# Rotating accumulator outputs, and sums and reciprocals planned apart, in a two-layer attention kernel

## The chip, the cores and the metric

The kernel runs on one core of one Trainium2 chip. The metric is the device time in microseconds of one launch. The core has five engines that run at the same time, each with its own queue of instructions in a fixed order: TensorE (PE) multiplies matrices, VectorE (DVE) and ScalarE (ACT) work on elements, GpSimd (POOL) too, and SyncE (SP) starts transfers. Semaphores tell one engine that another has finished, and an engine can also wait on its own.

## The reference

The input x has 8 batches of 1024 tokens (64 by 16) with 128 channels. Two layers follow each other.

```python
# layer 0: 8 heads; the softmax over m, then another one over g, of the same scores
scores = einsum('bhlfc,bhmgc->bhlfmg', q, k) / sqrt(c)
a = softmax(scores, axis=4)
a = softmax(a, axis=5)
z = einsum('bhlfmg,bhmgc->bhlfc', a, v)
z1 = layer_norm(z @ wo.T + bo + x)
x = layer_norm(relu(z1 @ w1.T + b1) @ w2.T + b2 + z1)
# layer 1, attention: additive scores, a tanh of every pair of tokens
Wi = B @ W.T                      # B: the normalised tokens
scores = einsum('d,bijd->bij', v, tanh(Wi[:, None] + Wi[:, :, None]))
t = t + softmax(scores, axis=-1) @ B
# layer 1, recurrence over the tokens
y_t = sigmoid(wx_t + y_{t-1} @ V)
```

The tanh of all pairs (1024 x 1024 x 128 for each of 8 batches, of which the symmetry lets the kernel compute about half) is the largest piece of work for ScalarE.

## The kernel before

Everything up to the recurrence is a list of operations, given to a small scheduler, the class `Plan`, which is part of the kernel's Python program. An operation has one or several engines that can do it, each with a price in microseconds written by hand (`add(("DVE", 1.49), first_sums, ...)`), the keys that it reads and writes, and a priority that acts as a due time in units of batches. `emit` runs through a simulated time and fixes, before anything runs on the chip, the order of each engine's instructions and, where there is a choice, the engine. At each step it takes the engine that can start first, at the time `first`, and then the operation of lowest priority value among those which can start on it by `first + slack`, with `slack=0.15`. An operation can start when its engine is free and all that it depends on is done, plus a delay: the table `LATENCY` if the other operation ran on another engine, the table `AGAIN` (line 500) if it ran on the same one.

Layer 0 works on tiles of 128 queries by 1024 keys, 64 tiles for each batch (8 heads by 8 tiles). The steps of a tile are: the scores on PE (L939) into one of two score buffers `sc`; the exponential on ACT (L942); on VectorE `first_sums`, one Python function with a `tensor_reduce` over m (L946) and a `reciprocal` of the 16 sums (L947); then `divide` (L950), which writes into a buffer `e` and sets the score buffer free. After each second tile there follow, for both together, the second exponential on ACT (L960), and on VectorE `second_sums`, with the reduction over g (L963) and a `reciprocal` of 128 sums (L964). GpSimd divides by them (L974), PE transposes (L853), VectorE copies the transposes out of PSUM (L865), and PE multiplies with the values (L988). There are two buffers `e` for pairs of tiles. `stat_e` holds the sums.

Layer 1's additive scores are computed in groups of rows (function `group`). A row is one token i against the tokens j: the matrix `wiT` plus one of its columns, then tanh, then a product with v on PE (L1175). ACT can do sum and tanh in one instruction for each row (L1097). Or GpSimd (L1107) or VectorE makes the sums, and ACT takes the tanh of many rows in one wide instruction (L1155). On VectorE a group of fewer than 4 rows is made row by row by `add_row` (L1101), a `tensor_scalar` with two additions and an accumulator output. That output is not used; it goes to `unused`, one column of the small tile `stats[5]`, the same for all rows. The scheduler chooses for each group which engine fills it; these rows are the work with which it fills ACT, VectorE and GpSimd. The sums lie in a ring in the tile `th`, whose room comes free when PE has used it.

Layer 0 of batch b+1 runs beside layer 1 of batch b, so that the first batch's layer 0 stands alone at first, and the last batch's layer 1 is alone at the end. After all batches the recurrence runs in chunks.

Of the kernel before, what the change touches and what calls it, by code (L numbers as in the profile page):

```python
# [11 lines left out]
ALU = mybir.AluOpType  # L12
# [3 lines left out]
P = 128  # L16
# [466 lines left out]
class Plan:  # L483
# [13 lines left out]


    LATENCY = {"PE": 0.6, "ACT": 0.5, "DVE": 0.4, "POOL": 0.6, "SP": 8.0}
    AGAIN = {"PE": 0.0, "ACT": 0.0, "DVE": 0.08, "POOL": 0.15, "SP": 8.0}  # L500

    def __init__(self):
        self.ops = []
# [130 lines left out]
def fast_path(ctx: ExitStack, tc: tile.TileContext, a: dict, fits):  # L634
# [22 lines left out]
    work = main.enter_context(tc.tile_pool(name="work", bufs=1))  # L657
    psum = main.enter_context(tc.tile_pool(name="psum", bufs=1, space=PSUM))

    def tile_of(pool, name, shape):  # L660
        return pool.tile(shape, F32, tag=name, name=name)
# [132 lines left out]
    add = plan.add  # L794
# [5 lines left out]
    stats = ring("stat", 7, [P, 4, 9])  # L800
# [36 lines left out]
    count = {"aT": 0}  # L837
# [34 lines left out]
    def layer0(b):  # L872
# [16 lines left out]
        for n_part, part in enumerate(parts):  # L889
# [3 lines left out]
            for h in range(H):  # L893
                L0 = pace(n_part, h)

                u, vp, kvp = us[h % 2], vps[h % 2], ("vp", h % 2)
                if alone:
                    vp, kvp = th[:, (12 + h) * N : (13 + h) * N].rearrange("p (t c) -> p t c", c=C), ("vp0", h)
                for s in range(2) if part is None else (part,):
                    cols = slice(s * 512, (s + 1) * 512)  # L900

                    def project(bank, h=h, cols=cols):
                        nc.tensor.matmul(bank, A[:, h, :], xT[:, cols], start=True, stop=True)  # L903

                    def biased(e, bank, h=h, u=u, cols=cols):
                        if e == "ACT":
                            nc.scalar.activation(u[:, cols], bank, AF.Identity, bias=ub[:, h : h + 1])
                        else:
                            nc.vector.tensor_scalar(u[:, cols], bank, ub[:, h : h + 1], None, ALU.add)

                    through_bank(project, 0.9, [kx], biased, evict(0.75), [], [("u", h % 2, s)], L0, banks)
                for s in () if alone and n_part else range(2):

                    def values(bank, h=h, s=s):
                        for i in range(4):
                            t = 4 * s + i
                            nc.tensor.matmul(  # L917
                                bank[:, i * P : (i + 1) * P], xT[:, t * P : (t + 1) * P], Wvo[:, h, :], start=True, stop=True
                            )

                    through_bank(
                        values, 0.95, [kx], copy(vp[:, 4 * s : 4 * s + 4, :]), evict(0.68), [], [kvp + (s,)], L0, banks
                    )
                for qt in qts:
                    L0 = pace(n_part, h + (qt - qts[0]) / len(qts))
                    i = (n_part * H + h) * len(qts) + qt - qts[0]
                    sc, kc = scs[i % 2], ("sc", i % 2)
                    pair, q = (b * H * NT + i) // 2 % NE, qt % 2
                    e2, st = es[pair], stat_e[pair]
                    e, ke = e2[:, q, :], ("e", pair, q)  # L930
                    k1, k2 = ke + (1,), ("e", pair, 2)
                    r1, r2 = st[:, q, 0:G], st[:, :, G : G + M]
                    sc3 = sc.rearrange("p (m g) -> p m g", g=G)
                    e3 = e.rearrange("p (m g) -> p m g", g=G)

                    def scores(_, sc=sc, u=u, qt=qt):
                        for s in range(2):
                            cols = slice(s * 512, (s + 1) * 512)
                            nc.tensor.matmul(sc[:, cols], u[:, qt * P : (qt + 1) * P], xT[:, cols], start=True, stop=True)  # L939

                    add(("PE", 1.74), scores, r=[kx, ("u", h % 2, qt // 4)], w=[kc], pri=L0)
                    add(("ACT", 0.98), lambda _, sc=sc: nc.scalar.activation(sc, sc, AF.Exp, scale=SCALE),  # L942
                        r=[kc], w=[kc], pri=L0)

                    def first_sums(_, sc=sc, r1=r1):
                        nc.vector.tensor_reduce(r1, sc.rearrange("p (m g) -> p g m", g=G), AX.X, ALU.add)  # L946
                        nc.vector.reciprocal(r1, r1)  # L947

                    def divide(_, e3=e3, sc3=sc3, r1=r1):
                        nc.vector.tensor_tensor(e3, sc3, r1.unsqueeze(1).to_broadcast([P, M, G]), ALU.mult)  # L950

                    add(("DVE", 1.49), first_sums, r=[kc], w=[k1], pri=L0)
                    add(("DVE", 1.22), divide, r=[kc, k1], w=[ke], pri=L0)
                    if q == 0:
                        continue


                    ks = [("e", pair, q) for q in range(2)]
                    L0 -= DOWN
                    add(("ACT", 1.9), lambda _, e2=e2: nc.scalar.activation(e2, e2, AF.Exp), r=ks, w=ks, pri=L0)  # L960

                    def second_sums(_, e2=e2, r2=r2):
                        nc.vector.tensor_reduce(r2, e2.rearrange("p q (m g) -> p q m g", g=G), AX.X, ALU.add)  # L963
                        nc.vector.reciprocal(r2, r2)  # L964

                    add(("DVE", 3.25), second_sums, r=ks, w=[k2], pri=L0)
                    na = next_aT()
                    aT = aTs[na]
                    for q in range(2):
                        e, ke = e2[:, q, :], ("e", pair, q)  # L970

                        def divide_again(_, e=e, r2=r2, q=q):
                            e3 = e.rearrange("p (m g) -> p m g", g=G)
                            nc.gpsimd.tensor_tensor(e3, e3, r2[:, q, :].unsqueeze(2).to_broadcast([P, M, G]), ALU.mult)  # L974

                        add(("POOL", 1.97), divide_again, r=[ke, k2], w=[ke], pri=L0)
                        for s in range(2):
                            through_bank(
                                transposes([e[:, t * P : (t + 1) * P] for t in range(4 * s, 4 * s + 4)]), 0.52, [ke],
                                copy(aT[:, 4 * s : 4 * s + 4, q * P : (q + 1) * P]), evict(0.68), [],  # L980
                                [("aT", na, q, s)], L0, banks,
                            )
                    q0 = (qt - 1) * P
                    bank = Bank(*banks)

                    def attend(part, vp=vp, aT=aT, bank=bank):
                        for t in range(4 * part, 4 * part + 4):
                            nc.tensor.matmul(bank()[:, :256], vp[:, t, :], aT[:, t, :], start=t == 0, stop=t == NT - 1)  # L988

                    def gather(_, h=h, q0=q0, bank=bank):  # L990
                        zq = zs[:, q0 : q0 + 2 * P]
                        if h == 0:
                            nc.vector.scalar_tensor_tensor(zq, bank()[:, :256], zb, xT[:, q0 : q0 + 2 * P], ALU.add, ALU.add)
                        else:
                            nc.vector.tensor_tensor(zq, bank()[:, :256], zq, ALU.add)

                    for s in range(2):
                        add(
                            ("PE", 1.74), lambda _, attend=attend, s=s: attend(s),
                            r=[kvp + (p,) for p in range(2)] + [("aT", na, q, p) for q in range(2) for p in range(2)],  # L1000
                            w=[("bank", bank)], pri=L0, take=None if s else bank, wait=[kz + (qt // 4,)],
                        )
                    add(("DVE", 0.42), gather, r=[("bank", bank), kx], w=[kz + (qt // 4,)], pri=L0, give=bank)

            L0 = b - 1 - SOON
            for qh in range(2) if part is None else (part,):
# [11 lines left out]
                z1T, k1 = zs[:, 512 * qh : 512 * qh + 512], kz + (qh,)  # L1018
# [51 lines left out]

                add(("POOL", 2.2), affine2, r=[kg], w=[kg], pri=L0)

    unused = stats[5][:, 3, 8:9]

    def group(it, at0, r0, k, wiT, all_wi, L1, ROWS, fillers, chain, left, both, first_half):

# [4 lines left out]
        i0 = it * P  # L1081
# [7 lines left out]
        def rows(c):  # L1089
            return slot()[:, at[c] : at[c + 1]].rearrange("p (r n) -> p r n", r=k)  # L1090

        def w_i(c, r=None):
            j = i0 + 4 * r0 + c
            return wiT[:, j : j + 4 * k - 3 : 4] if r is None else wiT[:, j + 4 * r : j + 4 * r + 1]
# [4 lines left out]
        def add_row(c, r):  # L1099

            nc.vector.tensor_scalar(  # L1101
                rows(c)[:, r, :], wiT[:, i0 + begin[c] :], w_i(c, r), 0.0, ALU.add, ALU.add, accum_out=unused
            )

        def add_rows(eng, c):
# [472 lines left out]
```

## Time and profile before

| | |
|---|---|
| median of 3 runs | 5390.36 us (5388.69 to 5394.67) |
| the profiled execution | 5390.73 us, its span 5388.9 us |
| reductions L946 / L963 | 512 x 1.212 us / 256 x 2.278 us |
| reciprocals L947 / L964 | 512 x 0.253 us / 256 x 0.953 us |
| divide L950 | 512 x 1.219 us |
| rows on VectorE, L1101 | 1822, mean 0.871 us, and an accumulator read of 0.083 us each |
| rows on ACT, L1097 | 2056, mean 0.782 us |
| wide tanh on ACT, L1155 | 971, mean 2.771 us |
| rows on GpSimd, L1107 | 2304 instructions, mean 1.486 us (VectorE has 80 of this line besides) |

A time in the profile is the time at which an engine worked on an instruction. The records of two instructions of one engine can overlap a little. "Idle before" is what lay free on the engine before an instruction starts, with the engine (and its line) whose signal ended the wait. A fixed order means that an engine whose next instruction waits does nothing else in the meantime.

### The profile page before, as it was taken

What the parts mean: (1) busy time and instruction counts of PE and PEld (TensorE: products, weight loads), DVE (VectorE), ACT (ScalarE), POOL (GpSimd) and SP (SyncE); (2) the same over time, 40 slices, a digit from 0 to 9 for tenths busy, and PEclk for the clock granted to TensorE, in tenths of its full rate; (3) what the DMA queues carried; (4) which work ended last, traced back from release to release, by engine and by line L of the source; (5) the groups of instructions that cost most, each with busy time, mean ns of one, the idle gap of its engine ahead of it and who ended that gap; (6) DMA issues with size and microseconds to landing.
All of it is one profiled execution on the core that took longest, in us unless ns stands there. A gap on an engine that the chain in (4) does not pass through costs nothing.

```text
span 5388.9 us, 99191 instructions
## 1 busy us (share of the span) xinstructions
PE 5048.0 (94%) x39173; PEld 2782.9 (52%) x39173; DVE 4961.5 (92%) x8448; ACT 5093.6 (95%) x4180; POOL 4536.0 (84%) x3114
## 2 busy tenths in 40 slices
PE   9999999999999999999999999999999999986567
PEld 6655555555555555555555555555555455542125
DVE  7998999999999999999999999999999999988886
ACT  5489999999999999999999999999999999999994
POOL 2364889988998899989999999989999998986992
PEclk9999999999999999999999999999999999998998
DMA  2000000000000000000000000000000000000001
GB/s 62 1 5 1 1 1 5 1 9 1 1 5 5 5 1 1 5 9 1 1 5 5 5 1 1 5 5 5 1 1 5 5 1 1 5 26 7 1 1 68
DMA packets 27339, 37.71 MB, mean 7 GB/s; under 512 B 2512, under 2 KB 19280, under 8 KB 26864
## 3 DMA queue, kind: packets, MB, share of 16 engines
q1 hardware_dynamic: 24832, 27.99, 1.6%
q8 instruction: 310, 5.08, 0.4%
q10 hardware_dynamic: 1872, 3.16, 0.2%
q14 instruction: 165, 1.35, 0.1%
q0 software_dynamic: 160, 0.13, 0.0%
HBM read 19.22 MB, written 12.06 MB: 6 GB/s over the span
## 4 chain that ended last, share of the span: by engine, by line
PE 67%; DVE 15%; ACT 12%; issue 4%; POOL 1%; DMA 0%; DVEq 0%; SPq 0%; ACTq 0%; POOLq 0%
PE sa L1175 24%; PE m L988 13%; PE sc L939 13%; PE m L853 8%; ACT th L1155 6%; DVE th L1101 6%; ACT th L1097 3%; DVE stat_e L963 2%; PE m L917 2%; PE m L1304 2%; DVE stat_e L946 2%; DVE wx L950 1%; PE m L903 1%; DVE aT L865 1%; PE m L1035 1%
## 5 line engine op out<-in xcount | busy, mean ns | idle before, releaser
L1107 POOL TENSOR_TENSOR th<-wiT 128x536 f32<-128x536 f32 (+58 forms) x2304 | 3342.3, 1486 | 244.6 <-PE sa L1175 222.8
L1155 ACT ACTIVATE th<-th 128x2740 f32<-128x2740 f32 (+54 forms) x971 | 2661.2, 2771 | 23.2 <-DVE th L1107 12.3
L1175 PE MATMUL sa<-th,vpat 128*32 128x512 f32 (+32 forms) x24576 | 2030.6, 462 | 212.5 <-ACT th L1155 187.2
L1101 DVE TENSOR_SCALAR_CACHE_REDUCE th<-wiT 128x512 f32<-128x512 f32 (+60 forms) x1822 | 1587.4, 871 | 140.1 <-PE sa L1175 21.9
L1097 ACT ACTIVATE th<-wiT 128x440 f32<-128x440 f32 (+58 forms) x2056 | 1462.7, 782 | 15.1 <-PE sa L1175 14.9
L1175 PEld LDWEIGHTS sa<-th,vpat 128*32 128x32 f32 x24576 | 662.1, 110 | 1341.8 <-issue 850.5
L974 POOL TENSOR_TENSOR wx<-wx,stat_e 128x1024 f32<-128x1024 f32 x512 | 983.2, 1942 | 403.5 <-DVE stat_e L964 360.4
L939 PE MATMUL sc<-xT,wx 128*128 128x512 f32 x2048 | 982.9, 605 | 15.7 <-DVE wx L950 15.3
L988 PE MATMUL m<-aT,wx 128*128 128x256 f32 x3584 | 829.4, 384 | 11.9 <-DVE aT L865 11.9
L988 PEld LDWEIGHTS m<-aT,wx 128*128 128x128 f32 x3584 | 671.1, 191 | 191.9 <-issue 40.7
L946 DVE TENSOR_REDUCE stat_e<-sc 128x16 f32<-128x1024 f32 x512 | 620.4, 1212 | 28.7 <-ACT sc L942 27.8
L950 DVE TENSOR_TENSOR wx<-sc,stat_e 128x1024 f32<-128x1024 f32 x512 | 623.9, 1219 | 23.3
L865 DVE COPY aT<-m 128x512 f32<-128x512 f32 x927 | 600.4, 674 | 34.5 <-PE m L853 32.1
L853 PEld LDWEIGHTS m<-ident,wx 128*128 128x128 f32 x3940 | 445.8, 141 | 326.0 <-issue 162.8
L963 DVE TENSOR_REDUCE stat_e<-wx 128x128 f32<-128x2048 f32 x256 | 583.3, 2278 | 19.0 <-ACT wx L960 18.1
L853 PE MATMUL m<-ident,wx 128*128 128x128 f32 x3940 | 564.4, 278 | 22.5 <-DVE aT L865 12.9
L942 ACT ACTIVATE sc<-sc 128x1024 f32<-128x1024 f32 x512 | 513.7, 1008 | 75.9 <-PE sc L939 71.0
L939 PEld LDWEIGHTS sc<-xT,wx 128*128 128x128 f32 x2048 | 354.9, 190 | 384.3 <-issue 331.4
L960 ACT ACTIVATE wx<-wx 128x2048 f32<-128x2048 f32 x256 | 487.2, 1903 | 21.6 <-DVE wx L950 21.3
L964 DVE RECIPROCAL stat_e<-stat_e 128x128 f32<-128x128 f32 x256 | 244.0, 953 | 8.8
L917 PEld LDWEIGHTS m<-Wvo,xT 128*128 128x128 f32 x1080 | 135.5, 193 | 47.5 <-issue 20.1
L917 PE MATMUL m<-Wvo,xT 128*128 128x128 f32 x1080 | 147.3, 282 | 6.4 <-DVE aT L865 3.0
(183 smaller groups left out, 2899.0 us busy)
## 6 DMA issues: line engine op xcount, KB each, us to landing
xT<-in_xt_dram SPq DMA_DIRECT2D x8, 512.0 KB, 3.5
th<-in_x_dram SPq DMA_DIRECT2D x8, 512.0 KB, 6.9
parked<-X SPq DMA_DIRECT2D x16, 256.0 KB, 2.3
xr<-parked SPq DMA_DIRECT2D x8, 512.0 KB, 7.7
parked_wx<-bT SPq DMA_DIRECT2D x14, 256.0 KB, 2.0
wx<-parked_wx SPq DMA_DIRECT2D x7, 512.0 KB, 3.2
out_dram<-ot ACTq DMA_DIRECT2D x8, 256.0 KB, 2.2
out_dram<-ot SPq DMA_DIRECT2D x8, 256.0 KB, 2.7
```

The source lines that it names most:

```text
L853: nc.tensor.transpose(bank[:, i * P : (i + 1) * P], s, ident)
L939: nc.tensor.matmul(sc[:, cols], u[:, qt * P : (qt + 1) * P], xT[:, cols], start=True, stop=True)
L946: nc.vector.tensor_reduce(r1, sc.rearrange("p (m g) -> p g m", g=G), AX.X, ALU.add)
L950: nc.vector.tensor_tensor(e3, sc3, r1.unsqueeze(1).to_broadcast([P, M, G]), ALU.mult)
L963: nc.vector.tensor_reduce(r2, e2.rearrange("p q (m g) -> p q m g", g=G), AX.X, ALU.add)
L974: nc.gpsimd.tensor_tensor(e3, e3, r2[:, q, :].unsqueeze(2).to_broadcast([P, M, G]), ALU.mult)
L988: nc.tensor.matmul(bank()[:, :256], vp[:, t, :], aT[:, t, :], start=t == 0, stop=t == NT - 1)
L1097: nc.scalar.activation(rows(c)[:, r, :], wiT[:, i0 + begin[c] :], AF.Tanh, bias=w_i(c, r))
L1101: nc.vector.tensor_scalar(rows(c)[:, r, :], wiT[:, i0 + begin[c] :], w_i(c, r), 0.0, ALU.add, ALU.add, accum_out=unused)
L1107: eng.tensor_tensor(rows(c), wiT[:, i0 + begin[c] :].unsqueeze(1).to_broadcast(shape), w_i(c).unsqueeze(2).to_broadcast(shape), ALU.add,)
L1155: nc.scalar.activation(slot()[:, a:z], slot()[:, a:z], AF.Tanh)
L1175: nc.tensor.matmul(sa[32 * c : 32 * c + 32, s:s1], vpat[:, 31 - r0 - r : 63 - r0 - r], rows(c)[:, r, s - at0 - begin[c] : s1 - at0 - begin ...
```

## The change

There are three edits. The accumulator outputs of `add_row` go to 16 columns of a new tile in turn. `first_sums` and `second_sums` each become two operations of the scheduler: the reduction, and the reciprocal that reads and overwrites its result; the prices become 1.15 + 0.2 for 1.49, and 2.2 + 0.9 for 3.25. The delay that the scheduler takes for an operation on VectorE which depends on another one on VectorE goes from 0.08 to 0.2.

```diff
-    AGAIN = {"PE": 0.0, "ACT": 0.0, "DVE": 0.08, "POOL": 0.15, "SP": 8.0}
+    AGAIN = {"PE": 0.0, "ACT": 0.0, "DVE": 0.2, "POOL": 0.15, "SP": 8.0}
...
                     def first_sums(_, sc=sc, r1=r1):
                         nc.vector.tensor_reduce(r1, sc.rearrange("p (m g) -> p g m", g=G), AX.X, ALU.add)
+
+                    def first_inverse(_, r1=r1):
                         nc.vector.reciprocal(r1, r1)
...
-                    add(("DVE", 1.49), first_sums, r=[kc], w=[k1], pri=L0)
+                    add(("DVE", 1.15), first_sums, r=[kc], w=[k1], pri=L0)
+                    add(("DVE", 0.2), first_inverse, r=[k1], w=[k1], pri=L0)
                     add(("DVE", 1.22), divide, r=[kc, k1], w=[ke], pri=L0)
...
                     def second_sums(_, e2=e2, r2=r2):
                         nc.vector.tensor_reduce(r2, e2.rearrange("p q (m g) -> p q m g", g=G), AX.X, ALU.add)
+
+                    def second_inverse(_, r2=r2):
                         nc.vector.reciprocal(r2, r2)
 
-                    add(("DVE", 3.25), second_sums, r=ks, w=[k2], pri=L0)
+                    add(("DVE", 2.2), second_sums, r=ks, w=[k2], pri=L0)
+                    add(("DVE", 0.9), second_inverse, r=[k2], w=[k2], pri=L0)
...
-    unused = stats[5][:, 3, 8:9]
+    unused = tile_of(work, "unused", [P, 16])
+
+    def next_unused():
+        count["unused"] = (count.get("unused", -1) + 1) % 16
+        return unused[:, count["unused"] : count["unused"] + 1]
...
             nc.vector.tensor_scalar(
-                rows(c)[:, r, :], wiT[:, i0 + begin[c] :], w_i(c, r), 0.0, ALU.add, ALU.add, accum_out=unused
+                rows(c)[:, r, :], wiT[:, i0 + begin[c] :], w_i(c, r), 0.0, ALU.add, ALU.add, accum_out=next_unused()
             )
```

## The prediction

> **What bounds the kernel now.** I read the page's busy shares first, then busy time by stage, then what ScalarE waits for in the longest stage, and last VectorE's instructions one by one. The first line of the page:
>
> ```profile
> PE 5048.0 (94%) x39173; PEld 2782.9 (52%) x39173; DVE 4961.5 (92%) x8448; ACT 5093.6 (95%) x4180; POOL 4536.0 (84%) x3114
> ```
>
> Three engines lie within three points of each other, so a mean over the span doesn't say which of them sets the end. The busy time by stage (stretch, its length, then busy us and instructions of PE, weight loads, DVE, ACT, POOL, clock, DMA) does:
>
> ```profile
> 100.00:400.00 300.00, 281.53 (x1330) 179.21 (x1329) 272.16 (x361) 189.05 (x211) 142.73 (x84) 0.99 0.01 3
> 400.00:700.00 300.00, 287.56 (x2094) 172.83 (x2093) 277.86 (x408) 291.73 (x420) 209.65 (x131) 0.99 0.00 1
> 700.00:1900.00 1200.00, 1160.74 (x8856) 635.12 (x8854) 1124.18 (x1824) 1159.99 (x846) 1066.00 (x731) 0.99 0.01 4
> 1900.00:4700.00 2800.00, 2745.94 (x21885) 1501.40 (x21882) 2644.51 (x4475) 2782.38 (x2073) 2592.13 (x1795) 1.00 0.01 3
> 4700.00:5200.00 500.00, 348.06 (x3309) 136.17 (x3311) 441.62 (x950) 489.86 (x314) 422.33 (x282) 0.93 0.03 11
> ```
>
> From 1900 to 4700 us ACT is busy 2782 of 2800 us (99.4%) and VectorE 94%; from 4700 to 5200 ACT 98%. ACT is the pacer there. Only before 400 us is ACT loose (63%), with PE at 94% and VectorE at 91%: there layer 0 of the first batch runs alone, and its chain of single steps counts. What ACT waited for in the long stage (line, releaser, total us, times, longest) leaves little to be won from VectorE directly:
>
> ```profile
> ACT sc L942 <- PE sc L939: 10.5, 13, 1.8
> ACT E L1271 <- PE sa L1175: 2.8, 3, 1.8
> ACT th L1097 <- PE sa L1175: 1.3, 2, 1.1
> ACT wx L960 <- DVE wx L950: 1.2, 2, 1.0
> ```
>
> VectorE's own time line (start, length, instruction, idle before) shows what the change aims at:
>
> ```profile
> 2516.51 0.08 DVE L1101 DVE_READ_ACCUMULATOR th<-wiT 128x1 f32 x1
> 2516.72 1.10 DVE L1101 TENSOR_SCALAR_CACHE_REDUCE th<-wiT 128x855 f32<-128x855 f32 x1
> 2517.75 0.08 DVE L1101 DVE_READ_ACCUMULATOR th<-wiT 128x1 f32 x1
> 2517.95 1.10 DVE L1101 TENSOR_SCALAR_CACHE_REDUCE th<-wiT 128x854 f32<-128x854 f32 x1
> 2518.98 0.08 DVE L1101 DVE_READ_ACCUMULATOR th<-wiT 128x1 f32 x1
> 2518.98 1.28 DVE L865 COPY wx<-m 128x512 f32<-128x512 f32 x2
> 2520.18 1.09 DVE L1101 TENSOR_SCALAR_CACHE_REDUCE th<-wiT 128x853 f32<-128x853 f32 x1
> 2521.20 0.08 DVE L1101 DVE_READ_ACCUMULATOR th<-wiT 128x1 f32 x1
> 2521.20 1.22 DVE L946 TENSOR_REDUCE stat_e<-sc 128x16 f32<-128x1024 f32 x1
> 2522.45 0.25 DVE L947 RECIPROCAL stat_e<-stat_e 128x16 f32<-128x16 f32 x1
> 2522.74 1.23 DVE L950 TENSOR_TENSOR wx<-sc,stat_e 128x1024 f32<-128x1024 f32 x1
> ```
>
> After an accumulator read a COPY or a reduction starts at the read's own start; the next row starts 0.20 to 0.21 us later. All rows write their accumulator to the one column `unused`, so each waits for the one before. The reduction, the reciprocal and the divide depend on each other too, and each starts about 0.035 us after its predecessor's end, where an independent instruction starts about 0.08 us before it (2520.18 against 2518.98 + 1.28).
>
> **What the Trainium skill says.** "VectorE: DVE Perf Modes", section "Two Vector instructions with no wait between them", counts an operation with accumulator output as two instructions; the trace agrees (1822 of each at L1101). The same page, section "The DRAIN you can't avoid", asks for a semaphore or an intervening operation where VectorE reads what it has just written, and says that the semaphore costs nothing extra. The first half fits the waits seen here. The second doesn't: 0.035 us after the end against 0.083 us before it is 0.118 us for each dependent pair, and the measurement decides. "Perfetto Trace Analysis", section "Tensor Engine Instruction (MATMUL, LD_WEIGHTS)", says that a matmul's end is estimated; so I don't take PE's 98% in the long stage as proof that PE is full.
>
> **Part 1, rotating outputs.** 1180 of the 1822 rows follow another row directly and wait on VectorE's own semaphore (counted over VectorE's records in order). Their starts lie after the accumulator read's end by 0.035 us (438 of them, that one wait), 0.12 (397, two waits) or 0.15 (344, three); without it I expect -0.083, as for the other instructions. Savings: 438 x 0.118 = 52, 397 x 0.216 (mean gap with the few true waits) = 86, 344 x 0.252 = 87: 224 us of VectorE time. A column comes round again after 16 rows, some 15 us later, so its wait costs nothing. Cover: all this is idle time of VectorE, which isn't the pacer after 400 us. The planner's row price (0.21 + 1.05e-3 w) isn't edited, so this part alone moves no row to another engine. Direct worth: nothing to ACT's load; ACT's waits on VectorE in 700 to 1900 us come to some 15 us (L1155 on L1107 9.8, on L1101 1.4, L960 on L950 3.8). I take -6, between 0 and -15.
>
> **Part 2, sums and reciprocals apart, dearer dependence.** The same instructions; L946 takes 1.212 us x512, L947 0.253 x512, L963 2.278 x256, L964 0.953 x256. With the planned delay of 0.2 us against a choice window of 0.15, the reciprocal can't be picked directly after its sums while another VectorE operation is ready. Every pair that is parted saves 0.118: 512 = 60 us; reciprocal to divide, 295 direct pairs now with 0.03 to 0.13 us gaps, 48 us; second sums, 256 = 30 us. At most 138 us of VectorE time, none where nothing else is ready.
>
> What reaches the end is the planner's new balance. It books 1.35 instead of 1.49 (512 x 0.14 = 72) and 3.10 instead of 3.25 (256 x 0.15 = 38): 110 us less on VectorE. It fills that with rows. A row taken from ACT saves ACT its fixed part only, since the tanh stays: seven rows of 610 took 4.93 us, 0.70 each; at 0.874 ns an element (L960 2048 in 1.903, L942 1024 in 1.008) 0.53 of that is the tanh, 0.17 the fixed part. For all engines to end dT earlier: rows off ACT dT/0.17 = 5.9 dT, rows off POOL dT/1.49 (L1107's mean) = 0.67 dT, each 0.95 us on VectorE (0.871 + 0.083), and VectorE itself dT shorter: 110 = dT(1 + 0.95 x 6.57) = 7.2 dT, dT = 15. The 0.08 us that the planner left idle after sums before is now filled: up to 41 us more, worth up to 6; I take 3. Sum -18; bounds 0 (all rows come off POOL) and -21.
>
> **The lone stage.** Up to 700 us there are 105 tiles. Two score buffers turn round there: a tile holds its buffer for 9.4 us (median, first score matmul to end of divide) of a cycle of 10.4 before 300 us, and 11.3 of 13.5 from 300 to 700; in the long stage only 9.1 of 17. Parting gives VectorE 0.36 us a tile (0.118, then 0.187 for the commonest gap of 0.104 before a divide plus 0.083, and half of 0.118), at best 49 x 0.36 = -18 in the part that VectorE helps to bound. But what is put between, mostly a COPY of 0.67 (0.60 with the overlap), lengthens the hold: twice 0.60 less 0.24 saved is +0.96, +0.48 a tile through two buffers, at worst 105 x 0.48 = +50. No row of before shows which wins; I take -2. Queued behind a delayed reciprocal is everything on VectorE; ACT's second exponential, PE's next scores and POOL's L974 (360 us of waits on L964 now, covered by POOL's slack) wait for it. No DMA, matmul or activation is added.
>
> Sum: -6 - 18 - 2 = -26 against the profiled 5390.7 (span 5388.9 and 1.8 around it) gives 5364.7; the median shown is 0.4 lower: 5364.
>
> **Rivals.** *VectorE's saving passes through.* The chain of waits gives VectorE 15% of the span, 808 us; shortened by 362 of 4961 (7.3%) that is -59: 5331. For it: PE waits on VectorE's copies in many small pieces. Against it: ACT's 99.4%. *Nothing arrives.* Rows come off POOL and the order reshuffles: 5390. For it: POOL has rows enough. *Slower: the score-buffer ring.* Place: layer 0 before 700 us, where hold almost equals cycle. Price: +0.48 us a tile, +50, less the 24 won later: 5416. It decides once the hold there rises by over 0.5 us (105 x 0.25 = 26, the whole gain). For it: the planner now prefers to put something between even if the tile is late. Against it: less queueing on a shorter VectorE. That the change misses its aim (waits stay since the tile and not the column is tracked) is unlikely: the reciprocal at L1308 writes the same tile as `unused` and starts directly after an accumulator read without that wait; it falls under "nothing arrives".
>
> **How the numbers follow.** Forecast 0.45 (own range 5345 to 5379), passes through 0.13, nothing 0.17, ring 0.25. Faster by over 0.2% (11 us, about what can be told from no change) 0.58, same 0.17, slower 0.25. The range takes the first rival's centre and reaches just past the ring's: 5325 to 5420.
>
> **What would show it.** Rows in sequence starting 0.08 us before the accumulator read's end; L947 seldom directly after L946; VectorE's busy share or its idle changed by 250 to 360 us in all; ACT still above 98% from 1900 us; fewer rows at L1097 than 2056 by about 90 (15/0.17). Wrong if ACT's rows don't fall, or if the hold of a score buffer before 700 us grows and ACT's full stretch begins later.

## The result and the profile after

The changed kernel takes 5317.8 us (median of 4, 5316.9 to 5319.5), 0.9869 of the kernel before (5389.5 with a fourth run; 95% interval 0.9857 to 0.9881): 72 us or 1.3% faster. The forecast was 5364, with a range from 5325. The direction was right; the gain was nearly three times the size, and the time lies 7 us below the range.

The busy line of the page after:

```profile
PE 5007.1 (94%) x39173; PEld 2763.8 (52%) x39173; DVE 4884.6 (92%) x8676; ACT 5057.1 (95%) x4042; POOL 4522.8 (85%) x3113
```

The span fell from 5388.9 to 5315.0, by 73.9 us. ACT's busy time fell by 36.5 (from 5093.6), and what is left of the span, ACT's idle time, by 37.4 (295.3 to 257.9). So, counted on ACT, half of the gain is less work and half is less waiting. VectorE's busy time fell by 77 us although it makes more rows; its share of the span is still 92%.

By stage (columns as before: stretch, length, busy us of PE, weight loads, DVE, ACT, POOL):

```profile
100.00:400.00 300.00, 276.71 (x1344) 177.77 (x1343) 276.16 (x395) 189.40 (x213) 148.73 (x87) 0.99 0.01 3
700.00:1900.00 1200.00, 1188.69 (x9224) 651.03 (x9216) 1129.55 (x1919) 1192.01 (x851) 1109.07 (x758) 1.00 0.01 4
1900.00:4700.00 2800.00, 2746.61 (x21924) 1501.89 (x21917) 2640.55 (x4659) 2779.45 (x2024) 2611.45 (x1812) 1.00 0.01 4
4700.00:5200.00 500.00, 329.15 (x3416) 119.35 (x3417) 430.57 (x1027) 499.55 (x267) 427.23 (x304) 0.97 0.02 7
```

ACT is full in more of the span: 1192 of 1200 us from 700 to 1900 (1160 before), and 499.6 of 500 after 4700 (489.9 before). The lone stage up to 400 us is as it was. The groups of rows moved like this (busy us, mean ns, then the idle time before them and what ended most of it); first VectorE's rows before, then the kernel after:

```profile
L1101 DVE TENSOR_SCALAR_CACHE_REDUCE th<-wiT 128x512 f32<-128x512 f32 (+60 forms) x1822 | 1587.4, 871 | 140.1 <-PE sa L1175 21.9
```

```profile
L1165 ACT ACTIVATE th<-th 128x2634 f32<-128x2634 f32 (+53 forms) x997 | 2734.8, 2774 | 9.3 <-DVE th L1117 6.0
...
L1111 DVE TENSOR_SCALAR_CACHE_REDUCE th<-wiT 128x344 f32<-128x344 f32 (+59 forms) x1930 | 1602.9, 867 | 68.6 <-PE sa L1185 65.8
L1107 ACT ACTIVATE th<-wiT 128x512 f32<-128x512 f32 (+62 forms) x1904 | 1369.8, 793 | 11.8 <-PE sa L1185 11.8
```

ACT does 1904 rows instead of 2056, VectorE 1930 instead of 1822. The idle time before VectorE's rows fell from 140.1 to 68.6 us, and what is left is nearly all a true wait on PE, which sets room in the ring free. VectorE's time line shows both aims of the change reached:

```profile
2503.99 1.23 DVE L946 TENSOR_REDUCE stat_e<-sc 128x16 f32<-128x1024 f32 x1
2505.13 0.94 DVE L969 RECIPROCAL stat_e<-stat_e 128x128 f32<-128x128 f32 x1
2505.99 0.20 DVE L949 RECIPROCAL stat_e<-stat_e 128x16 f32<-128x16 f32 x1
2506.11 0.98 DVE L1111 TENSOR_SCALAR_CACHE_REDUCE th<-wiT 128x829 f32<-128x829 f32 x1
2507.01 0.09 DVE L1111 DVE_READ_ACCUMULATOR th<-wiT 128x1 f32 x1
2507.10 0.42 DVE L1001 TENSOR_TENSOR zs<-m,zs 128x256 f32<-128x256 f32 x1
2507.44 1.22 DVE L952 TENSOR_TENSOR wx<-sc,stat_e 128x1024 f32<-128x1024 f32 x1
...
2521.92 1.05 DVE L1111 TENSOR_SCALAR_CACHE_REDUCE th<-wiT 128x818 f32<-128x818 f32 x1
2522.90 0.08 DVE L1111 DVE_READ_ACCUMULATOR th<-wiT 128x1 f32 x1
2522.90 1.06 DVE L1111 TENSOR_SCALAR_CACHE_REDUCE th<-wiT 128x817 f32<-128x817 f32 x1
```

Another reciprocal stands between the reduction at 2503.99 and its own at 2505.99, two other operations before its divide, and every instruction starts at or before its predecessor's end. The row at 2522.90 starts with the accumulator read of the row before it. The reduction L946 is followed directly by its reciprocal 48 times of 512, and L966 3 times of 256.

### The profile page after: what moved, and what is told of

It reads as the page before. It is cut to its first block, busy times and chain, and to the rows that moved or that the text cites. A ratio compares the mean times of both kernels' runs of the same rounds, so it can differ in the third digit from the quotient of the medians.

```text
span 5315.0 us, 98773 instructions
## 1 busy us (share of the span) xinstructions
PE 5007.1 (94%) x39173; PEld 2763.8 (52%) x39173; DVE 4884.6 (92%) x8676; ACT 5057.1 (95%) x4042; POOL 4522.8 (85%) x3113
## 4 chain that ended last, share of the span: by engine, by line
PE 67%; ACT 16%; DVE 10%; issue 6%; POOL 1%; DMA 0%; ACTq 0%; DVEq 0%; SPq 0%; POOLq 0%
PE sa L1185 25%; PE m L994 13%; PE sc L939 13%; ACT th L1165 9%; PE m L853 8%; ACT th L1107 4%; DVE th L1111 2%; PE m L1314 2%; PE m L917 2%; DVE stat_e L966 2%; PE m L903 1%; DVE stat_e L946 1%; ACT wx L963 1%; ACT sc L942 1%; DVE aT L865 1%
## 5 line engine op out<-in xcount | busy, mean ns | idle before, releaser
L1117 POOL TENSOR_TENSOR th<-wiT 128x1024 f32<-128x1024 f32 (+59 forms) x2303 | 3345.5, 1487 | 215.2 <-PE sa L1185 196.0
L1165 ACT ACTIVATE th<-th 128x2634 f32<-128x2634 f32 (+53 forms) x997 | 2734.8, 2774 | 9.3 <-DVE th L1117 6.0
L1185 PE MATMUL sa<-th,vpat 128*32 128x512 f32 (+36 forms) x24576 | 2009.0, 459 | 202.2 <-ACT th L1165 186.9
L1111 DVE TENSOR_SCALAR_CACHE_REDUCE th<-wiT 128x344 f32<-128x344 f32 (+59 forms) x1930 | 1602.9, 867 | 68.6 <-PE sa L1185 65.8
L1107 ACT ACTIVATE th<-wiT 128x512 f32<-128x512 f32 (+62 forms) x1904 | 1369.8, 793 | 11.8 <-PE sa L1185 11.8
L865 DVE COPY aT<-m 128x512 f32<-128x512 f32 x940 | 616.6, 684 | 67.6 <-PE m L853 64.3
L946 DVE TENSOR_REDUCE stat_e<-sc 128x16 f32<-128x1024 f32 x512 | 613.5, 1204 | 38.9 <-ACT sc L942 37.7
L966 DVE TENSOR_REDUCE stat_e<-wx 128x128 f32<-128x2048 f32 x256 | 583.6, 2280 | 52.5 <-ACT wx L963 51.9
L1111 DVE DVE_READ_ACCUMULATOR th<-wiT 128x1 f32 x1930 | 160.8, 83 | 0.0
```

Source lines behind the costliest of these rows:

```text
L865: nc.vector.tensor_copy(dst, src)
L1107: nc.scalar.activation(rows(c)[:, r, :], wiT[:, i0 + begin[c] :], AF.Tanh, bias=w_i(c, r))
L1111: nc.vector.tensor_scalar(rows(c)[:, r, :], wiT[:, i0 + begin[c] :], w_i(c, r), 0.0, ALU.add, ALU.add, accum_out=next_unused())
L1117: eng.tensor_tensor(rows(c), wiT[:, i0 + begin[c] :].unsqueeze(1).to_broadcast(shape), w_i(c).unsqueeze(2).to_broadcast(shape), ALU.add,)
L1165: nc.scalar.activation(slot()[:, a:z], slot()[:, a:z], AF.Tanh)
L1185: nc.tensor.matmul(sa[32 * c : 32 * c + 32, s:s1], vpat[:, 31 - r0 - r : 63 - r0 - r], rows(c)[:, r, s - at0 - begin[c] : s1 - at0 - begin ...
```

## The experiments

The theories: W, the waits of the rows are the gain; P, the scheduler's new order is, by its lower prices or by the parting; D, the longer delay alone is; and, after the first set of runs, L, much of it is the luck of one order among many. A number in the name of a "delay" or "reroll" kernel is the same-engine delay for VectorE. The kernel before was run again beside each set, with medians from 5384.4 to 5389.5 us; each ratio is to the median of its own set.

**Each part alone.** `rotate_only` is the kernel before with the rotating outputs alone, so its order is that of before. `plan_only` is the changed kernel with a single column again.

```diff
# rotate_only, against before
-    unused = stats[5][:, 3, 8:9]
+    unused = tile_of(work, "unused", [P, 16])
-  accum_out=unused
+  accum_out=next_unused()
# plan_only, against the changed kernel: the same lines the other way round
```

> Only the accumulator outputs rotate; the order of every engine stays that of the kernel before. Theory P (the gain is the scheduler's new order): VectorE isn't the pacer, so this is worth little, 5380 to 5390. Theory W (the gain is the waits of the rows that go away): most of the 72 us come here, 5325 to 5345, and ACT's idle in 700 to 1900 us falls from 40 to about 10 us. My prediction's term for it was -6, so 5384.

> The order of the changed kernel, with all rows writing one accumulator column as before. Theory P: 5318 to 5335. Theory W: the waits come back and with them most of the time, 5365 to 5385. If the two parts simply add, the gain here and that of rotate_only sum to 72 us; if the order needs the shorter rows to be kept, they sum to clearly less.

Measured: `rotate_only` 5371.8 us, ratio 0.9968 (0.9955 to 0.998), 16 us off; `plan_only` 5333.4, 0.99 (0.9883 to 0.9916), 55 off. The two add up to the 72, and the rotation is worth the same 16 us in both orders (5333.4 to 5317.8). `plan_only` lies within P's 5318 to 5335. For the rotation neither number was met: W's is too large, P's near zero too small. VectorE's rows in `rotate_only`:

```profile
2500.01 0.08 DVE L1105 DVE_READ_ACCUMULATOR th<-wiT 128x1 f32 x1
2500.01 1.10 DVE L1105 TENSOR_SCALAR_CACHE_REDUCE th<-wiT 128x861 f32<-128x861 f32 x1
2501.04 0.08 DVE L1105 DVE_READ_ACCUMULATOR th<-wiT 128x1 f32 x1
2501.15 1.11 DVE L1105 TENSOR_SCALAR_CACHE_REDUCE th<-wiT 128x856 f32<-128x856 f32 x1
```

The first row starts with the accumulator read before it; the second starts a tenth of a microsecond after its read's start, since a wait on PE is still there. Over the 1180 pairs the sum of the gaps goes from +127 to -32 us: 158 us of VectorE time, not the 224 that I had reckoned. Most of what VectorE won became waiting for others. Its rows and its copies out of PSUM, in `rotate_only` (before, 21.9 us of the idle time before the rows was ended by PE, as shown above) and then the copies before:

```profile
L1105 DVE TENSOR_SCALAR_CACHE_REDUCE th<-wiT 128x512 f32<-128x512 f32 (+60 forms) x1822 | 1500.9, 869 | 78.4 <-PE sa L1179 75.7
L865 DVE COPY aT<-m 128x512 f32<-128x512 f32 x927 | 601.4, 675 | 66.4 <-PE m L853 63.3
```

```profile
L865 DVE COPY aT<-m 128x512 f32<-128x512 f32 x927 | 600.4, 674 | 34.5 <-PE m L853 32.1
```

ACT's idle time fell by 7 us from 700 to 1900 us (40 to 33) and by 8 after 4700 (10 to 2). The second is seen in what ACT waited for from 4600 to 5300 us, before and then in `rotate_only`:

```profile
ACT th L1155 <- DVE th L1101: 5.7, 11, 1.4
ACT E L1271 <- PE sa L1175: 3.8, 3, 2.1
ACT th L1155 <- DVE th L1107: 2.5, 2, 1.5
```

```profile
ACT E L1275 <- PE sa L1179: 3.0, 3, 1.3
ACT th L1159 <- POOL th L1111: 0.4, 1, 0.4
ACT th L1159 <- DVE th L1105: 0.2, 1, 0.2
```

With layer 0 gone, the rows of the last batch follow each other on VectorE, and ACT waited 8.2 us on them (the first and the third line); it hardly does any more. ACT's busy time is nearly the same (5090.2): no row changed engine.

**Price, parting and delay.** All three have rotating outputs.

```diff
# prices_only, against rotate_only
-  add(("DVE", 1.49), first_sums, ...)
+  add(("DVE", 1.35), first_sums, ...)
-  add(("DVE", 3.25), second_sums, ...)
+  add(("DVE", 3.1), second_sums, ...)
# delay_only, against rotate_only
-  "DVE": 0.08
+  "DVE": 0.2
# split_no_delay, against the changed kernel
-  "DVE": 0.2
+  "DVE": 0.08
```

> The kernel before with rotating outputs and only the two prices lowered (1.49 to 1.35, 3.25 to 3.10), sums and reciprocals still one operation each. By my sum the lower booking alone moves rows from ACT to VectorE worth 15 us against rotate_only, with about 90 rows fewer on ACT. If rows don't move, it equals rotate_only; if the parting is what counts, also.

> Rotating outputs and the same-engine delay of 0.2; sums and reciprocals one operation each, old prices. It compares with rotate_only (5372). Theory D (the delay alone, which keeps the divide from following its sums at once, gives the time): 5335 to 5350. Theory P (parting sums and reciprocal with lower prices is needed): 5365 to 5375. It could also lose, since the planner then leaves VectorE idle for 0.2 instead of 0.08 where nothing else is ready.

> The change, but with the same-engine delay left at 0.08, which lies inside the choice window of 0.15, so that sums and reciprocal may again follow each other. Theory P in the form that parting them matters: 5335 to 5360, since up to 138 us of VectorE's waits come back. If the new prices (110 us less booked on VectorE) do it: 5315 to 5325. Theory W: 5315 to 5325 as well, since the rows rotate.

Measured: `prices_only` 5354.9 (0.9937, 0.992 to 0.9953), `delay_only` 5339.6 (0.9917, 0.99 to 0.9933), `split_no_delay` 5368.3 (0.9963, 0.9949 to 0.9977). The prices alone give 17 us against `rotate_only` where my sum had put 15, but with 180 rows fewer on ACT, not 90. The delay alone, which cuts the divides directly behind their reciprocals from 295 to 64, gives 32: theory D's 5335 to 5350. `split_no_delay`, with the same lower prices and some pairs parted (386 of 512 first pairs and 119 of 256 second ones still direct), gains almost nothing and misses all three of its expectations. Theory D fits these last two; with `prices_only` beside them no sum of mechanisms fits all three, which raised the question of chance.

**Re-rolls.** The list scheduler answers a small change of one of its numbers with another order of some 99,000 instructions. The four `reroll` kernels are `rotate_only` with other delays inside the choice window of 0.15; the five `delay` kernels with a number are the changed kernel with other delays above it. (Theory P is met by `delay_018`, `delay_022` and `delay_025`, and missed by `delay_016`, `delay_030`, `reroll_006` and `reroll_010`. `reroll_012` lies inside the range for the mechanism, `reroll_004` 3 us above it.)

```diff
# reroll_004, _006, _010, _012, against rotate_only
-  "DVE": 0.08
+  "DVE": 0.04   # or 0.06, 0.1, 0.12
# delay_016, _018, _022, _025, _030, against the changed kernel
-  "DVE": 0.2
+  "DVE": 0.16   # or 0.18, 0.22, 0.25, 0.3
```

> The changed kernel with the delay at 0.16 instead of 0.2, still just over the choice window of 0.15. Theory P (being over the window is what counts): within 10 us of the changed kernel's 5318, and sums directly before reciprocals about as seldom (48 of 512). If the 54 us between rotate_only and the changed kernel were mostly a lucky order, this one should fall anywhere between 5320 and 5370.

> rotate_only with the delay at 0.06 instead of 0.08, both inside the window: no mechanism of any theory, only another order of the same operations. The spread against rotate_only (5372) is what a new order alone can do. Theory P: within 10 us of 5372. Theory L (luck of the order): off by 20 or more.

> As reroll_006 with the delay at 0.10. Theory P: within 10 us of 5372. Theory L: off by 20 or more in either direction.

> The changed kernel with the delay at 0.18. Delays of 0.16 (5355) and 0.2 (5318) part the sums from their reciprocals alike, yet lie 37 us apart, so a sample of such orders is needed. Theory P: parted orders lie below the unparted ones (5372, 5357, 5351), so under 5345 in most. Theory L: anywhere between 5318 and 5372.

> As delay_018 with 0.25. Theory P: under 5345. Theory L: anywhere between 5318 and 5372.

> As delay_018 with 0.3. Theory P: under 5345, perhaps a little later than 0.2, since the planner books more idle time. Theory L: anywhere between 5318 and 5372.

> rotate_only with the delay at 0.04. If parted orders are better by mechanism: near the mean of the unparted ones (5372, 5357, 5351), so 5350 to 5372. If all is chance: as likely under 5340 as above.

> rotate_only with the delay at 0.12, still inside the window. As reroll_004: 5350 to 5372 by mechanism, as likely under 5340 by chance alone.

> The changed kernel with the delay at 0.22. Parted orders so far: 5355, 5343, 5318, 5321, 5352. Mechanism: 5318 to 5355, with ACT's busy time between 5043 and 5064 as in the others, against 5084 to 5090 in unparted orders with the old prices. Chance alone: up to 5372.

Measured (median us; ACT busy, and span less ACT busy, of the profiled execution, which in `reroll_004` was 10 us faster and in `delay_025` 10 us slower than the median):

| delay | unparted, old prices | ACT busy / idle | delay | parted, new prices | ACT busy / idle |
|---|---|---|---|---|---|
| 0.04 | 5375.1 | 5085.3 / 277.7 | 0.16 | 5355.3 | 5064.4 / 291.1 |
| 0.06 | 5357.4 | 5083.8 / 274.2 | 0.18 | 5343.4 | 5053.9 / 287.7 |
| 0.08 | 5371.8 | 5090.2 / 279.7 | 0.2 | 5317.8 | 5057.1 / 257.9 |
| 0.10 | 5350.8 | 5089.3 / 259.4 | 0.22 | 5321.8 | 5050.7 / 272.7 |
| 0.12 | 5363.9 | 5090.7 / 270.3 | 0.25 | 5320.7 | 5043.1 / 285.9 |
| | | | 0.30 | 5351.7 | 5052.8 / 297.1 |
| mean | 5363.8 | 5087.9 / 272.3 | mean | 5335.1 | 5053.7 / 282.1 |

What the other two edits, lower prices with the parting and the longer delay, do together is in the means: 29 us. The scatter (standard deviations 10 and 17 over 5 and 6 orders) leaves this difference uncertain by about 8 (its standard error). ACT has 34 us less to do on average, without overlap between the two columns, and idles somewhat more. The changed kernel is the best of its six, 17 below their mean, by ACT's idle time; the order of before is the second worst of its five, 8 above theirs. So theory P holds for the sign and about half of the 54 us between `rotate_only` and the changed kernel. The other half is which order came out. That it is luck, theory L, is not shown for all of it: in the right half of the table the three delays from 0.2 to 0.25 lie within 4 us of each other and the others 22 us or more above, as they would if such a delay were the best one. One order at each delay can't tell this from chance. In the left half neighbours lie 13 to 21 us apart, up and down, and there chance is the plainer reading.

**Price against parting, a second order.** `prices_010` is `reroll_010` with the prices of `prices_only`.

> reroll_010 (5351) with the two prices lowered, unparted. If the lower booking is what moves rows off ACT: ACT busy near 5063 as in prices_only, and a time some 15 us under reroll_010, 5336, give or take the scatter. If it is the parting: ACT busy near 5085 and no gain.

Measured: 5343.4 (0.9915, 0.9895 to 0.9934), 7 us under `reroll_010` (13 by the two ratios); ACT busy 5074.9, halfway between the two expectations. The two orders with new prices and no parting average 5349.2, 15 under the old prices. But `split_no_delay` has the new prices and a short delay too; with it the average is 5355.5, only 8 under, and `delay_only`, with old prices, lies 24 under. So how the 29 us divide between prices, parting and delay stays open. ACT's busy time scatters less: 5087.9 on average with old prices and a short delay, 5070.0 in the three orders with new prices and a short delay, 5075.4 in `delay_only`, 5053.7 with all. So both the prices and the delay take work off ACT.

**The row's own price.** The planner books a row on VectorE at 0.21 + 1.05e-3 w, which is now above what it takes.

```diff
# row_price, against the changed kernel
-  "DVE": lambda c: (k * (0.21 + 1.05e-3 * (w - begin[c])), ...
+  "DVE": lambda c: (k * (0.13 + 1.05e-3 * (w - begin[c])), ...
```

> The changed kernel with the planner's price of a row on VectorE lowered by 0.08 (0.21 to 0.13 + 1.05e-3 w), which is nearer to what the chip takes now that the rows follow each other without a wait. If the planner's balance sets the end, VectorE takes more rows, ACT some 100 fewer, and by the sum of the prediction (1930 x 0.08 = 154 us booked less, over 7.2) about 20 us come off: 5297. If VectorE's slack on the chip is needed to keep ACT fed, no gain or a loss: 5318 to 5340.

Measured: 5315.0 (0.9864, 0.9848 to 0.9881), the same as the changed kernel. Its busy line:

```profile
PE 5012.0 (94%) x39173; PEld 2768.7 (52%) x39173; DVE 4983.3 (94%) x9016; ACT 5033.2 (95%) x3917; POOL 4482.2 (84%) x3085
```

ACT lost 24 us of work, about as reckoned (148 rows less), and got 23 us of idle time in its place. Of this 16 us are waits of its second exponential on VectorE's divide, in the changed kernel and then here:

```profile
ACT wx L963 <- DVE wx L952: 15.6, 12, 3.4
```

```profile
ACT wx L963 <- DVE wx L952: 31.5, 15, 6.0
```

That the busier VectorE costs what the lighter ACT gains would fit this. But the idle time of ACT is 280.6 us here, as in the average parted order (282.1); it was the changed kernel that had little. Against the mean of its kind, 5335.1, `row_price` is 20 us faster, just what was reckoned. One order doesn't decide between the two readings.

**A cause of the scatter.** In `delay_016` ACT's wide tanh waited far more than in the changed kernel (9.3 us):

```profile
L1165 ACT ACTIVATE th<-th 128x4096 f32<-128x4096 f32 (+50 forms) x996 | 2715.8, 2759 | 36.2 <-DVE th L1117 26.5 <-DVE th L1111 5.4 <-POOL th L1117 3.8
```

L1117 on VectorE is the instruction that makes four or more rows at once, with two inputs from SBUF. Five of its 89 took 4 to 11 us there. In the kernel before one such instruction looks like this, with GpSimd's rows beside it and ACT's wait behind it:

```profile
1247.82 10.95 DVE L1107 TENSOR_TENSOR th<-wiT 128x752 f32<-128x752 f32 x1
```

```profile
1243.81 14.16 POOL L1107 TENSOR_TENSOR th<-wiT 128x862 f32<-128x862 f32 x10
```

```profile
1258.87 2.72 ACT L1155 ACTIVATE th<-th 128x3024 f32<-128x3024 f32 x1 [6.82 <-DVE th L1107]
```

The median of the 80 is 1.08 us. The planner keeps these apart from GpSimd's work in its own simulated time, but on the chip they meet: 51 of the other 79 run beside GpSimd's additions for more than half of their time. The last two kernels make such rows one by one, and the planner's rule that keeps them apart (`port`) goes with them.

```diff
# rows_single, against the changed kernel; rows_single_016, against delay_016
   "DVE": lambda c: (k * (0.21 + 1.05e-3 * (w - begin[c])), lambda: [add_row(c, r) for r in rows_of])
-  if k < 4
-  else (0.15 + 1.04e-3 * k * (w - begin[c]), lambda: add_rows(nc.vector, c)),
...
-  port=k >= 4,
+  port=False,
```

> The changed kernel with VectorE's rows always one by one, never several in one instruction with two SBUF inputs (80 such instructions in the changed kernel, 106 us), and without the planner's rule that these don't run beside GpSimd. If their stalls beside GpSimd cost time: ACT's waits on them (6 us here) go, 5305 to 5318. As single rows they cost VectorE more each (0.21 fixed for each row), so if VectorE's load in the narrow groups counts: 5318 to 5335.

> delay_016 (5355) with rows one by one. If the stalls made that order bad (five over 3 us, ACT waits of 26.5 us on them): 5320 to 5335. If the scatter has other causes: 5335 to 5360.

Measured: `rows_single` 5307.3 (0.9854, 0.9835 to 0.9873), 11 us under the changed kernel, though the two intervals overlap; `rows_single_016` 5315.9 (0.9872, 0.9852 to 0.9891), 39 us under `delay_016`. In the latter the wide tanh waits no more:

```profile
L1163 ACT ACTIVATE th<-th 128x4096 f32<-128x4096 f32 (+51 forms) x980 | 2686.8, 2769 | 0.9 <-DVE th L1111 0.4 <-POOL th L1117 0.3
```

ACT's idle time fell from 291.1 to 245.8 us (5314.1 less 5068.3) and is 243.4 in `rows_single` (5305.4 less 5062.0), lower than in any other order. The waits of the wide tanh are 35 of these 45 us, and between the changed kernel and `rows_single` 7 of 14.5. That the stalls made ACT wait is shown by these lines; how much of the 39 and the 11 us is the stalls is not separated from the draw of two more orders, nor from the planner's freedom without its rule: GpSimd made 49 and 48 more of its additions there. And the stalls are not the only cause of the scatter: in `prices_only` no such instruction took over 2.8 us, and ACT idled 291.4 us.

## Why the prediction was wrong

- *ACT is the pacer after 400 us.* It stands: ACT is busy for 99% of the time from 700 to 5200 us, and of 158 us taken off VectorE 16 arrived, while VectorE waited more. (That the span's change is ACT's work plus ACT's idle time proves nothing; it holds for every engine.) The rival in which VectorE's saving passes through had the nearest number, 5331. At its own rate, 59 us for 362, the 158 us would be worth 26; the interval of `rotate_only` is 11 to 24. So its rate is too high for the rotation, but no further off than my 6.
- *Part 1, -6.* Mis-sized: 16 measured, twice. Its upper bound of 15 came from ACT's waits between 700 and 1900 us alone; I left out the last batch, where VectorE's rows stand in sequence and ACT waited 8.2 us on VectorE. The saving on VectorE was put too high: I let every pair close up, but with its own waits gone VectorE comes earlier, and 84 of the pairs then wait on PE. The sign of 250 to 360 us in VectorE's busy and idle time was not met: 77 us less busy and 3 more idle, with 108 rows more.
- *Part 2, -18 within 0 and -21.* For the whole part the orders show -29 with an error of 8, so it was probably too small, and the bound too tight. The term for the lower prices, 15, is neither confirmed nor refuted: 15 from two orders, 8 from three. The parting and its delay got 3, as filled idle time in the planner's balance; `delay_only`, 24 under the mean without it and with 12 us less work for ACT, says that this was too little. ACT's rows fell by 152, not 90; by the 0.17 us of a row's fixed part that is 26 of the 36.5 us that ACT does less, as an estimate.
- *The lone stage, -2.* Near nothing, as forecast: a tile holds its buffer for 9.9 us instead of 9.4 before 300 us and for 11.3 as before from 300 to 700; ACT's first scores' exponential of layer 1 starts at 424 us in both. The ring rival fell: its point of decision, half a microsecond more hold over all 105 tiles, was not reached.
- *The waits stay since the tile is tracked.* This fell, as argued from L1308: the rows of `rotate_only` start with the accumulator read.
- *The step that failed.* The sum took a changed order to give its mechanism's mean. It had no term for which order comes out, and for this scheduler orders of one kind lie 10 to 17 us (standard deviation) around their mean. The parts with their measured sizes, 16 and 29 in place of 6 and 18, give 45, so 5345, within the range. The changed kernel lies 17 below the mean of its kind and the order of before 8 above that of its own; these 25 us, uncertain by the same 8, carried the time out of a range that held unknown costs alone. No term of the prediction stood for them. Whether all of them are luck, or the delay of 0.2 is better than its neighbours for a reason, stays open.

## What to carry to other kernels

Where instructions write a result that nobody reads, give them several places in turn: here an engine paid for each wait on itself. And where a list scheduler fixes the order before the run, run the same mechanism in several orders by moving a number that should matter little: the scatter between them tells how much of one result belongs to the idea. This holds for a change that seems to gain nothing too: compare it with the mean of its kind, and not with one lucky kernel.

## What the runs showed of the hardware

A dependence between two neighbouring VectorE instructions cost 0.118 us (start 0.035 after the end against 0.083 before it), and up to 0.23 where the next instruction waited for two more semaphores; with rotating outputs the same rows start with the accumulator read. And a VectorE addition with two SBUF inputs, about 1 us long, took up to 14.9 us (`reroll_004`) beside a stretch of GpSimd's additions. Over all kernels with such instructions 38 of 1418 took over 3 us, each beside GpSimd's additions for over 70% of its time; of the 513 that ran beside them for less than a tenth, none took over 1.23 us. The Trainium skill says in "GPSIMD Engine Reference", section "Specifications", that GpSimd's SBUF interfaces are shared with VectorE and that instructions with two SBUF inputs contend; these traces fit that, with 3 to 15 us for the longest.
